# Third-level products in five more places, and the mixed kernels' operations handed out by a table

## The chip, the cores and the metric

The kernel runs on one core of one Trainium2 chip. The metric is the device time of one launch in microseconds (us); a core's engines are TensorE (PE for its matmuls, PEld for its weight loads), VectorE (DVE), ScalarE (ACT), GpSimd (POOL) and SyncE (SP, which here only issues transfers).

## The reference

Two layers work on `x` (32 samples, 128 channels, length 2048), all in float32:

```python
x = x + L0_ffn(L0_cond(x, cond))       # mixes channels per sample, then a 2048 x 2048 linear map along the length
x = x + L1_ffn(L1_cond(x, cond))       # grouped convolution of 9 taps, then 16 heads of up, gelu, down on permuted positions

# L0_cond:  att = softmax(mlp(cond));  out_b = (sum_k att[b,k] * weight[k]) @ x_b + att @ bias_k
# L0_ffn:   out = x @ W.T + bias + sum_e coeffs[e]*scales[e] * (x @ A[e].T) @ Bf[e].T
# L1_cond:  conv1d(x, weight, groups=4, padding=4) + cond @ c_weight.T + bias
# L1_ffn:   t = x[:, perm] as 16 heads of 128;  t = gelu(t @ up) @ down;  inverse permutation
```

The part that matters here is the linear map: 4096 rows (sample and channel) by 2048 by 2048, with the low-rank update folded into the weights first. Mixing the channels and the map along the length act on different axes, so the kernel does the map first and mixes its result. The mixing matrix of a sample (128 x 128, a sum of 8 given ones weighted by `att`) is its *mixed kernel*.

## The kernel before, in words

**Two levels of products, and a third in places.** The large product is done with the seven-product scheme (four sums of each operand, seven products P1 to P7, in place of eight). On the outside the 4096 rows are 8 groups `g` of 512, and each group's rows, the 2048 inputs and the 2048 outputs are halved. `ROUNDS` gives the order of the seven outer products: P1, P2, P6, P7, P5, P3, P4. A round keeps one set of weights (`rhs`) and goes through the eight groups; a step is one (round, group), and there are 56. In a step the same scheme is used again: 256 rows by 1024 by 1024 in seven products, each of 128 rows, 512 inputs and 512 outputs: four matmuls of 128 x 512, accumulated in a bank of PSUM. `multiply` (L341) does this. After each inner product DVE adds the bank to one or two places of the step's sum, `accs`, which is loaded from and stored to DRAM (`part_load`, `part_store`; `ADDED` says which sums a round adds to: two in P5, one in the others). Because a product accumulates onto a bank that held an earlier one (P6 and P7 on P1's, P3 on P5's), PE can start it only when DVE has read the bank.

**Third level.** For a pair of steps (g even, then g odd) listed in `PAIRS`, the inner products P2 and P4 of both steps are taken together: 256 rows by 512 by 512, done by seven *quarters*, each for P2 and P4 at once: four matmuls of 128 x 256 into the two halves of a bank (28 half-wide matmuls where 16 wide ones were). `multiply_third` (L575) does such a step; the even step leaves P2 and P4 out, the odd one has all the quarters. In the rounds of `ENDS` (P1 and P4) the quarters come behind the step's own products, otherwise among them. `MORE` lists pairs that do the same with the inner P3 and P7 (a second *family* of quarters): `multiply_more` (L482). There the even step already does P1 and P2 of both families, and the odd step the other ten quarters, the last ones in the order P7 of the second family, P4 of the first, P3 and P4 of the second. A quarter of the first family costs DVE one add of two halves (128 x 2 x 256) for each sum, one of the second also one of 128 x 256 (L527, L532).

**Inputs of the quarters.** `third_weights` (L388) makes eight sums of the weights on POOL and four on DVE (`quarter_ops`, done at points of the next steps); `more_weights` (L444) eight on POOL and eight on DVE (`more_ops`). `third_inputs` (L422) makes four sums of the two steps' x (two at once, two left in `rest` for later, if it runs on DVE); `more_inputs` (L463) four on POOL.

**Order of work.** The engines' queues are written by hand (`manual_schedule`), in the loop over `steps` (L1222). Before a step's matmuls come its loads, POOL's sums for the next step (`x_combine`), the loads of the next sums, and the weights of the next round (`outer_weights`, `inner_weights`). Inside a step six *points*, `between(0)` to `between(5)` (L1287), hang other work between the products; in the even step of a second-family pair, point 2 is behind P6 and points 3 to 5 among the quarters, in the odd step likewise. What hangs there: at points 0 to 3 of a step two of a mixed kernel's eight operations (`mixed_kernel`, L712 and L714, on DVE: 128 x 128, result = given matrix x att + result), one sample per step, in steps 6 and 7 of the first round and 1 to 6 of the later ones; at points 0 to 3 the waiting `quarter_ops` and `more_ops`; in the first round the row sums of the weights (`row_sums`, and for the first four weight tiles two adds at point 5 of each step). In the first round the other weights are also made, two tiles ahead of a step (`w_make_two`, L218).

**Buffers.** All large tiles share one pool of 26 slots of 1 MB (`SLOTS`); a load waits until its slot is free, and loads stand in one queue on SP. PSUM has 8 banks, taken and given back in turn.

In the last round (P4) the second layer begins between the products; after it PE runs the heads (L986, L997) to the end.

Of the kernel before, what the change touches and what calls it, by code (L numbers as in the profile page):

```python
# [48 lines left out]


PAIRS = {
    "P1": (1, 2, 3), "P2": (0, 1, 2, 3), "P6": (0, 1, 2, 3), "P7": (0, 1, 2, 3),
    "P5": (0, 1, 2, 3), "P3": (0, 1, 2, 3), "P4": (0,),
}
MORE = {"P7": (1, 2), "P3": (1, 2)}
ENDS = ("P1", "P4")
EARLY = 2

# [2 lines left out]
def adaln_ffn_kernel(  # L61
# [357 lines left out]

    rest = []  # L420

    def third_inputs(i, eng):  # L422

        (x11, x12), (x21, x22) = (
            [xa[n][:, 1, :, h * NQ : (h + 1) * NQ] for h in range(2)] for n in (i, i + 1)
        )
        tt = eng.tensor_tensor
        t = slot(f"sq_{i}", (P, 4, 2, NQ))
        tt(t[:, 0], x21, x22, ALU.add)
        tt(t[:, 1], t[:, 0], x11, ALU.subtract)  # L430
        rest.append((t[:, 2], x11, x21))
        rest.append((t[:, 3], x12, t[:, 1]))
        if eng is nc.gpsimd:
            sums_rest(eng)
        return {
            "P1": x11, "P2": x12, "P3": t[:, 3], "P4": x22,
            "P5": t[:, 0], "P6": t[:, 1], "P7": t[:, 2],
        }

    def sums_rest(eng):  # L440
        while rest:
            eng.tensor_tensor(*rest.pop(0), ALU.subtract)

    def more_weights(name, rhs):  # L444

# [36 lines left out]
    def multiply_more(r, g, lhs, rhs, accs, between, families):  # L482

        px, py = bank(), bank()
        if g % 2 == 0:
            both = [accs]
            held.extend((both, {}, {}))
        both, *sums = held
        if g % 2:
            both.append(accs)  # L490

        def add(ps, *to):
            for si, oi in to:
                for acc in accs:
                    nc.vector.tensor_tensor(acc[:, si, oi], ps, acc[:, si, oi], ALU.add)  # L495

        def product(k, ps, first, last):
            for kc in range(4):
                nc.tensor.matmul(  # L499
                    ps, lhsT=lhs[k][:, bass.ts(kc, P)], rhs=rhs[k][kc],  # L500
                    start=first and kc == 0, stop=last and kc == 3, skip_group_check=True,
                )

        def quarter(n, k):

            quarters, x = families[n]
            qs = sums[n]
            if k in ("P1", "P5", "P2"):
                qs[k] = bank()
            ps = qs[{"P6": "P1", "P7": "P1", "P4": "P1", "P3": "P5"}.get(k, k)]  # L510
            first, last = k in ("P1", "P2", "P5"), k in ("P2", "P3", "P4")
            for i, out in enumerate(halves(ps)):
                for kc in range(2):
                    nc.tensor.matmul(  # L514
                        out, lhsT=x[k][:, 1 - i if n else i, bass.ts(kc, P)],
                        rhs=quarters[i][k][kc],
                        start=first and i == 0 and kc == 0, stop=last and i == 1 and kc == 1,
                        skip_group_check=True,
                    )
            b, h = {  # L520
                "P1": (0, 0), "P2": (0, 0), "P6": (0, 1), "P5": (1, 1), "P7": (1, 1),
                "P3": (0, 1), "P4": (1, 0),
            }[k]
            cols = slice(h * NQ, (h + 1) * NQ)
            for acc in both[b]:
                part = acc[:, :, n, cols]
                nc.vector.tensor_tensor(  # L527
                    part, ps.rearrange("p (s n) -> p s n", s=2), part, ALU.add
                )
                if n:  # L530
                    part = acc[:, 1, 0, cols]
                    nc.vector.tensor_tensor(part, ps[:, NQ : 2 * NQ], part, ALU.add)  # L532
            if last:
                done(ps)

        def quarters_of(*nks):
            if g % 2:
                for n, k in nks:
                    quarter(n, k)

        product("P1", px, True, False)
        add(px, (0, 0))
        between(0)
        quarters_of((0, "P6"), (0, "P5"))
        product("P5", py, True, True)
        add(py, (1, 1), (0, 1))
        done(py)
        between(1)
        quarters_of((1, "P6"), (0, "P7"))
        product("P6", px, False, True)  # L550
        add(px, (0, 1), (1, 1), (1, 0))
        done(px)
        between(2)
        if g % 2 == 0:
            quarter(0, "P1")
            quarter(0, "P2")
            between(3)
            quarter(1, "P1")
            between(4)
            quarter(1, "P2")  # L560
            between(5)
            return
        quarters_of((1, "P5"), (0, "P3"))
        between(3)
        quarters_of((1, "P7"), (0, "P4"))
        between(4)
        quarters_of((1, "P3"))
        between(5)
        quarters_of((1, "P4"))
        held.clear()  # L570
        for b, accs in enumerate(both):
            for (_, new), acc in zip(ADDED[r], accs):
                part_store(new, g - 1 + b, acc, nc.sync)
# [639 lines left out]
    olds = {}  # L1213
    chain = small()
    nxt, waiting, ts, quarter_ops, more_ops = {}, {}, {}, [], []
    heads = [(g, h) for g in range(NG) for h in range(NH)]

    def olds_load(i):
# [3 lines left out]
    for i, (r, g) in enumerate(steps):  # L1222
        ri = i // NG
        last_round = ri + 1 == len(ROUNDS)
        if i + 1 < len(steps):
            if i + 1 not in xs:
                xs[i + 1] = x_loads(*steps[i + 1])
            if not last_round:
                lhs[i + 1] = x_combine(*steps[i + 1], xs.pop(i + 1))
                if g == 2 * PAIRS[r][0]:  # L1230
                    quarters, quarter_ops = third_weights(r, rhs)
                if in_pair(r, g) and g % 2 == 0 and g > 0 and r != "P6":
                    sq = third_inputs(i, nc.gpsimd)
                    if in_more(r, g):
                        sv = more_inputs(i)
                if r in MORE and g == 2 * MORE[r][0] - 1:
                    more, more_ops = more_weights(r, rhs)
        if i == 0:
# [48 lines left out]
        def between(j):  # L1287

            if j == 3 and 0 <= k_early < EARLY:
                outer_sums(k_early, early_x)  # L1290

            b = (ri - 1) * (NG - 2) + g + 1 if ri > 0 else g - (NG - 2)
            if (g in range(1, NG - 1) if ri > 0 else g >= NG - 2) and b < B:
                k = j - 2 if r == "P5" and g == 1 else j
                if 0 <= k < KEXP // 2:
                    mixed_kernel(b, (2 * k, 2 * k + 1))
            if ri == 0 and j == 2:
                for k in blocks[6 + 2 * g : 8 + 2 * g]:
                    wt[k] = w_load(*k)
            if j < 4 and quarter_ops:  # L1300
                nc.vector.tensor_tensor(*quarter_ops.pop(0), ALU.subtract)
            if j < 4 and more_ops:
                nc.vector.tensor_tensor(*more_ops.pop(0), ALU.subtract)
            if i == NG - 1 and j == 3:
                olds_load(i + 1)
            if j == 3 and ahead and steps[i + 2][0] == "P6":
                xs[i + 2] = x_loads(*steps[i + 2])
            if ri == 0 and j in (1, 3) and unsummed:
                row_sums(*unsummed.pop())
            if ri == 0 and j == 5 and unsummed_first:  # L1310
                t = unsummed_first.pop(0)
                tt = nc.vector.tensor_tensor
                tt(wsum[:, 0, 0], wsum[:, 0, 0], t[:, 0, 0], ALU.add)
                tt(wsum[:, 0], wsum[:, 0], t[:, 1], ALU.add)
            if last_round:
                if j == 1 and i + 1 < len(steps):
                    lhs[i + 1] = x_combine(*steps[i + 1], xs.pop(i + 1))
                    olds_load(i + 1)
                if j == 4 and i + 2 < len(steps):
                    xs[i + 2] = x_loads(*steps[i + 2])  # L1320
                if j in (2, 4):
                    stage(k0 + j // 2, stage_first)
                if j % 2:
                    stage_third(k0 + j // 2)
                else:
                    stage(k0 + j // 2, stage_second)
# [10 lines left out]
            multiply(r, g, lhs.pop(i), rhs, olds.pop(i), between)  # L1337
        xa.pop(i - 1, None)
        ss.pop(i - 1, None)
        if in_pair(r, g) and g % 2 == 0 and (g == 0 or r == "P6" or last_round):  # L1340
            sq = third_inputs(i, nc.gpsimd if r in ENDS else nc.vector)
        next(chain, None)
        if i > 4:
# [6 lines left out]
        if g == NG - 1 and ri + 1 < len(ROUNDS):  # L1350
            rhs = nxt
            nxt = {}

    before = None
    for k, (g, h) in enumerate(heads):
# [83 lines left out]
```

## Time and profile before

| | us |
|---|---|
| three runs | 2575.98, 2577.21, 2579.15 (median 2577.21) |
| the profiled execution | 2577.27 |
| its span, first to last instruction | 2575.5 |
| PE busy | 2564.0 |
| DVE busy | 1579.5 |
| POOL busy | 1394.2 |
| ACT busy | 532.3 |

The profile's lines name an engine, a line of the kernel, the tiles as output<-input, and counts. A group's line ends with its busy time, the mean of one instruction in ns and the idle time before it. In the timeline the first number is the start from the span's beginning, the second the time to the end of the last of the merged instructions, and what stands in brackets at the end is the idle time before and who ended it. Each matmul of float32 leaves two records there (7142 for 3571 instructions). The granted TensorE clock was 0.999 of full over the execution.

The rounds stand in the trace at these times: P1 from 45.9 us, P2 from 296.4, P6 from 482.8, P7 from 669.4, P5 from 853.1, P3 from 1038.8, P4 from 1222.5. An even step of a pair takes 17.2 us, an odd one 29.3 (27.6 to 28.9 with a second family).

### The profile page before, as it was taken

The numbers are of one execution on the slowest core, as the hardware profiler recorded it, in microseconds if no ns is written. First come the engines' busy times: TensorE is split into PE (matmuls) and PEld (weight loads), VectorE is DVE, ScalarE is ACT, GpSimd is POOL, SyncE is SP. The second block draws the span as 40 slices with busy tenths as digits, with TensorE's granted clock in tenths as the row PEclk, the third lists the DMA queues.
The fourth block names the chain that finished last, engine by engine and source line by source line (L and its number), as shares of the span: only waits on it lengthen the run. The fifth ranks groups of instructions, "written<-read, shape, count | busy, mean of one in ns | idle before, by whom it ended". The sixth has DMA issues, their size and how long they took to land.

```text
span 2575.5 us, 22121 instructions
## 1 busy us (share of the span) xinstructions
PE 2564.0 (100%) x7142; PEld 1355.4 (53%) x7142; DVE 1579.5 (61%) x2450; ACT 532.3 (21%) x1099; POOL 1394.2 (54%) x1158
## 2 busy tenths in 40 slices
PE   9999999999999999999999999999999999999999
PEld 4455555555566555566554554455555554455543
DVE  5665576666585576675476666666666666667611
ACT  0000000000000000000011244444444444444432
POOL 7431788878997736989432134444344434434222
PEclk9999999999999999999999999999999999999999
DMA  7452588579366486574866887787777877777432
GB/s 322 182 211 113 198 338 344 212 285 370 151 249 263 196 337 273 221 287 168 281 230 210 279 290 266 224 259 230 226 223 234 252 246 223 222 251 237 164 123 90
DMA packets 186867, 610.42 MB, mean 237 GB/s; under 512 B 17664, under 2 KB 91904, under 8 KB 142336
## 3 DMA queue, kind: packets, MB, share of 16 engines
q1 hardware_dynamic: 147936, 473.48, 51.2%
q0 software_dynamic: 32992, 132.14, 15.2%
q10 hardware_dynamic: 5824, 3.40, 0.5%
q8 instruction: 57, 0.93, 0.1%
q14 instruction: 58, 0.48, 0.1%
HBM read 372.45 MB, written 202.94 MB: 223 GB/s over the span
## 4 chain that ended last, share of the span: by engine, by line
PE 95%; DVE 3%; DMA 2%; issue 0%; SPq 0%; POOLq 0%; ACT 0%; ACTq 0%; DVEq 0%
PE bank L594 26%; PE bank L986 17%; PE bank L997 17%; PE bank L607 9%; PE bank L357 7%; PE bank L842 6%; PE bank L750 4%; PE bank L499 3%; PE bank L223 3%; PE bank L514 2%; DMA w<-in_WT 1%; DVE ags L714 1%; DMA xt<-in_xT 0%; DVE u L527 0%; DVE u L495 0%
## 5 line engine op out<-in xcount | busy, mean ns | idle before, releaser
L986 PE MATMUL bank<-t,ws 128*128 128x512 f32 x1024 | 460.3, 592 | 0.0
L997 PE MATMUL bank<-gl,ws 128*128 128x512 f32 x1024 | 460.1, 592 | 0.0
L1004 POOL DMA_INDIRECT out<-t,orow x128 | 152.3, 1189 | 535.8 <-DVE t L1002 452.5
L989 ACT ACTIVATE gl<-bank 128x512 f32<-128x512 f32 x512 | 306.1, 598 | 433.3 <-PE bank L986 414.1
L997 PEld LDWEIGHTS bank<-gl,ws 128*128 128x128 f32 x1024 | 194.6, 190 | 232.9 <-issue 231.5
L986 PEld LDWEIGHTS bank<-t,ws 128*128 128x128 f32 x1024 | 194.6, 190 | 226.6 <-issue 222.2
L594 PE MATMUL bank<-P_t,s_P 128*128 128x512 f32 x640 | 284.3, 592 | 0.4 <-ACT m_P L589 0.4
L1002 DVE TENSOR_TENSOR t<-bank,t 128x512 f32<-128x512 f32 x128 | 88.4, 690 | 320.2 <-PE bank L997 309.4
L735 POOL TENSOR_TENSOR x<-x,fb 128x512 f32<-128x512 f32 x128 | 174.5, 1392 | 198.9 <-DMA x<-in_x 136.4
L741 ACT ACTIVATE bank<-w,aggb 128x512 f32<-128x512 f32 x128 | 80.8, 684 | 880.3 <-DMA w<-w_d 867.8
L283 POOL TENSOR_TENSOR xt<-xt,xt 128x512 f32<-128x512 f32 x120 | 159.0, 1358 | 104.6 <-DMA xt<-in_xT 88.4
L714 DVE SCALAR_TENSOR_TENSOR ags<-mix,att_bc,ags 128x128 f32<-128x128 f32 x224 | 195.5, 873 | 4.7
L594 PEld LDWEIGHTS bank<-P_t,s_P 128*128 128x128 f32 x640 | 121.4, 190 | 140.4 <-issue 136.6
L587 DVE TENSOR_TENSOR u<-bank,u 128x512 f32<-128x512 f32 x156 | 101.6, 686 | 147.4 <-PE bank L594 135.1
L594 PE MATMUL bank<-wo_P,s_P 128*128 128x512 f32 x416 | 184.7, 592 | 0.0
L319 POOL TENSOR_TENSOR s_P<-xt 128x512 f32<-128x512 f32 x52 | 68.8, 1323 | 204.0 <-DMA xt<-in_xT 164.2
L970 POOL DMA_INDIRECT t<-hx_d,row x128 | 131.1, 1025 | 56.6 <-issue 25.6
L587 DVE TENSOR_TENSOR p<-bank,p 128x512 f32<-128x512 f32 x96 | 64.6, 687 | 117.8 <-PE bank L594 117.1
L594 PEld LDWEIGHTS bank<-wo_P,s_P 128*128 128x128 f32 x416 | 79.0, 190 | 89.2 <-issue 87.3
L842 PE MATMUL bank<-va,tw_l 128*128 128x256 f32 x512 | 121.5, 380 | 0.7 <-DVE va L826 0.7
L853 ACT ACTIVATE cv<-bank,ctxb 128x128 f32<-128x128 f32 x256 | 73.0, 368 | 234.6 <-PE bank L842 234.6
L753 DVE TENSOR_TENSOR x<-bank,x 128x512 f32<-128x512 f32 x128 | 88.1, 690 | 50.8 <-POOL x L735 21.9
(242 smaller groups left out, 3869.0 us busy)
## 6 DMA issues: line engine op xcount, KB each, us to landing
xt<-in_xT SPq DMA_DIRECT2D x84, 1024.0 KB
u<-u_d SPq DMA_DIRECT2D x40, 1024.0 KB
wo_P<-wb_d SPq DMA_DIRECT2D x36, 1024.0 KB
u<-c_d SPq DMA_DIRECT2D x64, 512.0 KB
x<-in_x SPq DMA_DIRECT2D x32, 1024.0 KB
xg<-x SPq DMA_DIRECT2D x256, 128.0 KB
hx_d<-x1t SPq DMA_DIRECT2D x32, 1024.0 KB
hx_d<-ht SPq DMA_DIRECT2D x32, 1024.0 KB
```

The source lines that it names most:

```text
L283: nc.gpsimd.tensor_tensor(out[:, i, j], a[:, i, j], b[:, i, j], op)
L357: nc.tensor.matmul(ps, lhsT=lhs[k][:, bass.ts(kc, P)], rhs=rhs[k][kc], start=first and kc == 0, stop=last and kc == 3, skip_group_check=True,)
L587: nc.vector.tensor_tensor(to, ps, to, ALU.add)
L594: nc.tensor.matmul(ps, lhsT=lhs[k][:, bass.ts(kc, P)], rhs=rhs[k][kc], start=first and kc == 0, stop=last and kc == 3, skip_group_check=True,)
L607: nc.tensor.matmul(out, lhsT=sq[k][:, i, bass.ts(kc, P)], rhs=quarters[i][k][kc], start=first and i == 0 and kc == 0, stop=last and i == 1 ...
L714: nc.vector.scalar_tensor_tensor(ag, mix[:, k], att, ag, ALU.mult, ALU.add)
L735: nc.gpsimd.tensor_tensor(xt[:, f], xt[:, f], late["fb"][:, f], ALU.add)
L842: nc.tensor.matmul(out, lhsT=w[:, 2 * i + r], rhs=rhs, start=first and r == 0, stop=last and r == 1, skip_group_check=True,)
L986: nc.tensor.matmul(pu, lhsT=w[:, m * P : (m + 1) * P], rhs=t[:, 0], start=True, stop=True)
L989: nc.scalar.activation(gl[m], pu, AF.Gelu)
L997: nc.tensor.matmul(pd, lhsT=w[:, (MC + m) * P : (MC + m + 1) * P], rhs=gl[m], start=(m == 0), stop=(m == MC - 1),)
L1004: nc.gpsimd.indirect_dma_start(out=out, out_offset=bass.IndirectOffsetOnAxis(ap=orow[:, g, h : h + 1], axis=0), in_=t[:, 1], in_offset=None,)
```

## The change

- `PAIRS`: P1's first pair (groups 0 and 1) now has the third level too, so all pairs of that round have it.
- `MORE`: a second family in one pair of P6 and of P5 (groups 2 and 3), and in the last pairs of P7 and P3 (groups 6 and 7), beside the two pairs each that P7 and P3 had.
- `MIXES`: the mixed kernels' operations are handed out by a table. For each round it has eight counts (operations per point in each of the eight groups) and eight first points; four points in a row get the count. The operations go in order through a list, `mixes`. The second-family pairs' even steps get 1 per point in place of 2 (none in P5's), the odd step of P5's pair 1 per point from point 2 on, and steps 7 of P2, P6, P7 and P5, which had none, 2 per point.
- `third_inputs`: all four sums go through `rest`; for P6's new pair none is made at once: two are made behind the even step, and two inside the odd step (`sums_rest`). Its input sums stay on DVE; `more_inputs` runs for the new pairs on POOL as for the old.
- In the first round, the row sums and the adds for the first four weight tiles stand at other points; the first pair's weight differences are made at step 0.

In the program that is 2306 matmuls of 128 x 512 in place of 2386, and 1318 of 128 x 256 in place of 1178; DVE has 42 more adds of 128 x 2 x 256, 51 more operations of 128 x 256 and two fewer of 128 x 512; POOL 20 more of 128 x 512 and 16 more of 128 x 256; SP's 742 transfers and the number of mixed-kernel operations stay.

```diff
 PAIRS = {
-    "P1": (1, 2, 3), "P2": (0, 1, 2, 3), "P6": (0, 1, 2, 3), "P7": (0, 1, 2, 3),
+    "P1": (0, 1, 2, 3), "P2": (0, 1, 2, 3), "P6": (0, 1, 2, 3), "P7": (0, 1, 2, 3),
     "P5": (0, 1, 2, 3), "P3": (0, 1, 2, 3), "P4": (0,),
 }
-MORE = {"P7": (1, 2), "P3": (1, 2)}
+MORE = {"P6": (1,), "P7": (1, 2, 3), "P3": (1, 2, 3), "P5": (1,)}
+MIXES = {
+    "P1": ((0,) * 8, (0,) * 8), "P2": ((0, 2, 2, 2, 2, 2, 2, 2), (0,) * 8),
+    "P6": ((0, 2, 1, 2, 2, 2, 2, 2), (0,) * 8), "P7": ((0, 2, 1, 2, 1, 2, 2, 2), (0,) * 8),
+    "P5": ((0, 2, 0, 1, 2, 2, 2, 2), (0, 2, 0, 2, 0, 0, 0, 0)),
+    "P3": ((0, 2, 1, 2, 1, 2, 2, 2), (0,) * 8), "P4": ((0,) * 8, (0,) * 8),
+}
...
-    def third_inputs(i, eng):
+    def third_inputs(i, eng, later=False):
...
-        tt(t[:, 0], x21, x22, ALU.add)
-        tt(t[:, 1], t[:, 0], x11, ALU.subtract)
-        rest.append((t[:, 2], x11, x21))
-        rest.append((t[:, 3], x12, t[:, 1]))
+        rest.append((t[:, 0], x21, x22, ALU.add))
+        rest.append((t[:, 1], t[:, 0], x11, ALU.subtract))
+        if not later:
+            sums_rest(eng, 2)
+        rest.append((t[:, 2], x11, x21, ALU.subtract))
+        rest.append((t[:, 3], x12, t[:, 1], ALU.subtract))
         if eng is nc.gpsimd:
             sums_rest(eng)
...
-    def sums_rest(eng):
-        while rest:
-            eng.tensor_tensor(*rest.pop(0), ALU.subtract)
+    def sums_rest(eng, n=4):
+        for _ in range(min(n, len(rest))):
+            eng.tensor_tensor(*rest.pop(0))
...
         quarters_of((0, "P6"), (0, "P5"))
+        if g % 2:
+            sums_rest(nc.vector)
         product("P5", py, True, True)
...
+    mixes = [(b, k) for b in range(2, B) for k in range(KEXP)]
...
-                if in_pair(r, g) and g % 2 == 0 and g > 0 and r != "P6":
-                    sq = third_inputs(i, nc.gpsimd)
-                    if in_more(r, g):
-                        sv = more_inputs(i)
+                if in_pair(r, g) and g % 2 == 0 and g > 0:
+                    if r != "P6":
+                        sq = third_inputs(i, nc.gpsimd)
+                    elif in_more(r, g):
+                        sq = third_inputs(i, nc.vector, True)
+                if in_more(r, g) and g % 2 == 0:
+                    sv = more_inputs(i)
...
-            if (g in range(1, NG - 1) if ri > 0 else g >= NG - 2) and b < B:
-                k = j - 2 if r == "P5" and g == 1 else j
-                if 0 <= k < KEXP // 2:
-                    mixed_kernel(b, (2 * k, 2 * k + 1))
+            if ri == 0 and g >= NG - 2 and j < KEXP // 2:
+                mixed_kernel(b, (2 * j, 2 * j + 1))
+            if 0 <= j - MIXES[r][1][g] < 4:
+                for _ in range(MIXES[r][0][g]):
+                    if mixes:
+                        b, k = mixes.pop(0)
+                        mixed_kernel(b, (k,))
...
-            if j < 4 and quarter_ops:
+            if i and j < 4 and quarter_ops:
...
-            if ri == 0 and j in (1, 3) and unsummed:
+            if ri == 0 and unsummed and (j in (1, 3) and (i, j) != (1, 3) or (i, j) == (3, 2)):
                 row_sums(*unsummed.pop())
-            if ri == 0 and j == 5 and unsummed_first:
+            if (i, j) in ((2, 5), (3, 0), (3, 4), (4, 0)) and unsummed_first:
...
-        if in_pair(r, g) and g % 2 == 0 and (g == 0 or r == "P6" or last_round):
+        if in_more(r, g) and r == "P6":
+            sums_rest(nc.vector, 2)
+        elif in_pair(r, g) and g % 2 == 0 and (g == 0 or r == "P6" or last_round):
             sq = third_inputs(i, nc.gpsimd if r in ENDS else nc.vector)
```

More of the change, by code (lines that the diff above doesn't have):

```diff
@@ L1352, in adaln_ffn_kernel @@
             nxt = {}
+    assert not mixes
     before = None
```

## The prediction

> **What bounds the kernel now.** First the page: its span, its busy line, and the chain that ended last.
>
> ```profile
> span 2575.5 us, 22121 instructions
> PE 2564.0 (100%) x7142; PEld 1355.4 (53%) x7142; DVE 1579.5 (61%) x2450; ACT 532.3 (21%) x1099; POOL 1394.2 (54%) x1158
> PE 95%; DVE 3%; DMA 2%; issue 0%; SPq 0%; POOLq 0%; ACT 0%; ACTq 0%; DVEq 0%
> ```
>
> TensorE is never out of work, so next what one matmul costs: the timeline of PE in a step of a pair with both families of quarters.
>
> ```profile
> 1102.43 3.60 PE L499 MATMUL bank<-wo_P,xt 128*128 128x512 f32 x8
> 1105.87 3.62 PE L514 MATMUL bank<-P_q,sq 128*128 128x256 f32 x16
> 1109.32 1.02 PE L499 MATMUL bank<-P_t,s_P 128*128 128x512 f32 x2
> ```
>
> A matmul leaves two records. From start to start eight wide records take 3.44 us and sixteen half-wide ones 3.45, so 0.859 us for a wide matmul and 0.431 for a half-wide one. The program's 2386 wide and 1178 half-wide matmuls make 2050 + 508 = 2558 us: only about 18 us of the span are anything else. Which waits these are, the PE's list of waits says:
>
> ```profile
> PE bank L514 <- DVE u L532: 1.1, 2, 0.8
> PE bank L514 <- DVE u L527: 0.5, 1, 0.5
> ```
>
> Both stand in pairs of this kind (starts late at 745.67, 760.10, 1128.50 and 1174.30; with the pipe's refill 0.75, 0.63, 0.33 and 1.02 us, 2.73 in sum). The last one, on DVE and then PE:
>
> ```profile
> 1164.95 1.88 DVE L495 TENSOR_TENSOR u<-bank,u 128x512 f32<-128x512 f32 x3 [1.53 <-PE bank L499]
> 1166.75 2.60 DVE L714 SCALAR_TENSOR_TENSOR ags<-mix,att_bc,ags 128x128 f32<-128x128 f32 x2
> 1169.27 0.68 DVE L527 TENSOR_TENSOR u<-bank,u 128x512 f32<-128x512 f32 x1
> 1169.87 0.41 DVE L532 TENSOR_TENSOR u<-bank,u 128x256 f32<-128x256 f32 x1
> 1170.20 0.68 DVE L527 TENSOR_TENSOR u<-bank,u 128x512 f32<-128x512 f32 x1
> 1170.80 2.51 DVE L714 SCALAR_TENSOR_TENSOR ags<-mix,att_bc,ags 128x128 f32<-128x128 f32 x2
> 1173.23 0.68 DVE L527 TENSOR_TENSOR u<-bank,u 128x512 f32<-128x512 f32 x1
> 1173.84 0.41 DVE L532 TENSOR_TENSOR u<-bank,u 128x256 f32<-128x256 f32 x1
> 1174.30 1.99 PE L514 MATMUL bank<-P_v,s_P 128*128 128x256 f32 x8 [0.76 <-DVE u L532]
> ```
>
> I call this the tail of an odd step. From P6's end PE has five quarters (8.6 us) until P4 of the second family needs its bank read; DVE has the adds of P6 and of three quarters (4.34 us by these cadences: 0.60, 0.60 and 0.33) and in between the mixed-kernel operations of two points, four of them here. These depend on POOL:
>
> ```profile
> 907.82 0.73 DVE L714 SCALAR_TENSOR_TENSOR ags<-mix,att_bc,ags 128x128 f32<-128x128 f32 x2
> 549.20 11.31 POOL L283 TENSOR_TENSOR xt<-xt,xt 128x512 f32<-128x512 f32 x8 [18.34 <-DMA xt<-in_xT]
> 920.05 4.99 POOL L283 TENSOR_TENSOR xt<-xt,xt 128x512 f32<-128x512 f32 x4 [23.40 <-DMA xt<-in_xT]
> ```
>
> At 907.8 POOL is idle and one costs 0.37 us; in the tail POOL runs one sum behind the other and one costs 1.24.
>
> **The change, part by part.** The profiled execution took 2577.27 us (its span and 1.77 around it), 0.06 over the median of the three runs, 2577.21; I sum against it.
>
> *Matmuls.* Five more uses of the third level: P1's first pair, and a second family in a pair of P6, P7, P5 and P3. Each drops 16 wide matmuls for 28 half-wide ones: 80 x 0.859 = 68.7 us against 140 x 0.4315 = 60.4. PE has **8.3 us** less.
>
> *DVE, P7 and P3.* The even steps of their old second-family pairs get 4 mixed-kernel operations in place of 8. In P7's step 3 DVE starts 5.4 us behind PE (P1's add begins at 741.85, its product ended at 736.4), the 0.75 us at 745.67. Four operations at 1.25 fewer take 5 us of that lag: **-0.75**. The odd steps keep eight, two per point, so the tails stay: 0.63, 0 (P7's step 5, where POOL paused and four cost 2.9), 0.33 and 1.02, a mean of 0.5. Such odd steps are now six (P6's 3, P7's 3, 5 and 7, P3's 3 and 5; P3's 7 has no mixed-kernel work): 6 x 0.5 = 3.0 in place of 1.98, **+1.0**. Ends: 0, if POOL pauses in each, and 1.1 each, if all four cost 1.27.
>
> *P5's pair.* Each add goes to two sums, so the tail's DVE work doubles: 6 x 0.60 + 1.87 + 1.2 + 1.87 + 0.1 = 8.6 us, which alone is over the 8.4 that PE leaves, plus two mixed-kernel operations (now one per point, from point 2). Stall 0.3 + 2m: 1.0 at m = 0.37, 2.8 at 1.27. In P5's step 3 the trace has POOL working through this stretch and eight of them took 8.8 us, so m = 1.1 and **+2.5**. Nearly all that this pair saves (1.66) is lost here. A rule of the Trainium skill (SBUF — State Buffer, Who interferes with whom: a VectorE instruction with two SBUF inputs and a GpSimd instruction that reads SBUF exclude each other, the second blocking until the first has finished) would make m a whole POOL sum, 1.27, and this +2.8; the trace's eight stay below it on the mean. Behind the pair DVE is some 4 us late in step 4, whose P6 waits only for P1's add, 6.9 us in: no cost.
>
> *P6's pair.* Its first two input sums are now queued on DVE behind the even step's last adds and needed 3.4 us into the odd step. Counting DVE's queue with four mixed-kernel operations and four weight differences (L1303: 1.48 beside POOL, 0.41 without), the adds end 0.9 us into the odd step and the sums (0.68 to 1.6 each) at 2.3 to 4.1: 0 to 0.7, taken 0, since POOL is idle there (18.34 us before 549.20).
>
> *P1.* Row sums leave point 5 of step 3, where they and the small chain delay the first adds of the weights (0.54 us at 181.42). One of two such waits goes (the other, 0.28 at 139.22, stays, as step 2 keeps its point 5): **-0.5**. Bounds: -0.8, and +1 for sums put in other places.
>
> *POOL* gets per new family 8 weight differences x 0.76 (P6 and P5 alone) and 4 input sums x 1.30: 11.2 us ahead of P7 and as much ahead of P3. It has the 18.3 and 23.4 us of waiting for loads shown above: nothing. *Queues*: the same 742 transfers leave SP; two more buffers in use in P6 and P5, and the quarters' in P1, make some loads start later. The tightest is a weight of P1 (w_111): its buffer now comes free with PE's step 1, about 15 us before its first add, where it was 35; a load into an idle queue (400's x: issued 139.9, first summed 145.3) took 5.4. The removed zero-mix steps (P2's, P6's, P7's, P5's step 7) have DVE at 9 to 18 of 29 us: 8 operations x 1.1 fit.
>
> Sum: -8.3 - 0.75 + 1.0 + 2.5 - 0.5 = -6.05: **2571.2 us**.
>
> **Rivals.**
>
> *All of it arrives.* POOL pauses in the tails and P5's two mixed-kernel operations cost 0.37: 1.0 + 6 x 0.33 in stalls, 3.0 against 2.73: -8.3 + 0.3 - 0.5 = -8.5, 2568.8. For it: P7's step 5. Against: three tails of four.
>
> *DVE's mixed-kernel work eats it.* Every one of these operations waits out a POOL sum, 1.27: six tails x 1.1 + 2.8 = 9.4 against 2.73, so -8.3 + 6.7 - 0.5 = -2.1, 2575.2. For it: the tail shown above; against: the other three (1.07, 1.06 and 0.73 each). It is what the Trainium skill's rule on the shared port (the page and section above) tends to where POOL's work has no gap; one tail of four agrees with it in full.
>
> *Slower: a half-wide matmul comes dearer than half.* Each needs its own weight load (190 ns against 216 ns of matmul). The place is the 140 new matmuls; it decides from 0.491 us on (68.7 / 140), and at three quarters of a wide one (0.64) they cost 90 us: +21 + 2.3, some 2600. Against it: the fence above, 0.431, with loads hidden. The Trainium skill (TensorE: Matmul & The Clock Gate, Back-to-back issue gap) states that in a stream of weight load and matmul the spacing falls from 131 ns at 512 columns only to 81 at 128, which would be such a price; this trace contradicts it, with 430 and 216 ns.
>
> *Slower: POOL's waits don't absorb its new work.* Then the 11.2 us come off POOL's lead on PE, which is 8.0 us at P7's step 1 and 6.2 at P3's (end of the weight difference to PE's first read): 3.2 + 5.0 lost, 2579.4, and over 2582 if POOL's sums run at 1.41 (the 11.31 us line) and not 1.27.
>
> **How the numbers follow.** The sum 0.50 (own range 2569.5 to 2573.5), all arrives 0.23, mixed-kernel work 0.18, dearer half-wide matmuls 0.02, POOL 0.07. A difference under 0.2%, 5.2 us, can't be told from none. Faster by more: 0.38 of the first and all of the second, 0.61; within: the rest of the first, the third, and 0.02 of POOL's, 0.32; slower 0.07. The range leaves out the two slower rivals and the ends of the others: 2567.5 to 2576.5.
>
> **What would show it.** PE's records: 2306 and 1318 matmuls, 0.859 and 0.431 us. No late start in P7's step 3 at the first family's P7; one of 1 to 3 us at the last quarter of P5's step 3; six tails of 0 to 1.1. POOL's gaps before P6's fourth and P5's third inputs shrunk by some 5 to 11 us. Wrong if PE waits for POOL or a load anywhere in P6 to P3, or if a tail costs over 3 us.

## The result, and the profile after

The changed kernel's median is 2573.2 us (22 runs, 2570.6 to 2575.0), that of the kernel before, beside it on the same chip, 2577.7 us: a ratio of 0.9982, 95% interval 0.9976 to 0.9988. It is faster, by 4.5 us: the interval leaves out 1, but the gain is a little less than the 0.2% (5.2 us) that the prediction set as its bound, so that its "faster by more", at 0.61, did not come, and its "within", at 0.32, did. Predicted were 2571.2 us and a range of 2567.5 to 2576.5, in which the time lies. The profiled execution took 2574.09 us against 2577.27, 3.2 less.

First the page: its span, its busy line and the chain that ended last.

```profile
span 2572.3 us, 22495 instructions
PE 2556.4 (99%) x7262; PEld 1377.8 (54%) x7262; DVE 1642.9 (64%) x2541; ACT 532.4 (21%) x1099; POOL 1435.0 (56%) x1194
PE 95%; DVE 4%; DMA 0%; issue 0%; POOLq 0%; ACTq 0%; ACT 0%; DVEq 0%
```

PE is still what fills the span; DVE has one per cent more of the chain than before. What a matmul costs has not moved, as PE's timeline in P3's step 3 shows (start, duration, line, matmul records):

```profile
1100.13 3.60 PE L507 MATMUL bank<-wo_P,xt 128*128 128x512 f32 x8
1103.57 3.62 PE L522 MATMUL bank<-P_q,sq 128*128 128x256 f32 x16
1107.02 3.60 PE L507 MATMUL bank<-P_t,s_P 128*128 128x512 f32 x8
```

Eight wide records again take 3.44 us from start to start and sixteen half-wide ones 3.45. The program has 2306 wide and 1318 half-wide matmuls. What changed is PE's list of waits; these four of its lines bear on the change (line, releaser: us in total, times, longest):

```profile
PE bank L522 <- DVE u L540: 2.1, 3, 1.0
PE bank L229 <- DVE w L232: 2.0, 1, 2.0
PE bank L507 <- DVE u L503: 1.5, 1, 1.5
PE bank L522 <- DVE p L540: 0.2, 1, 0.2
```

The first and last lines are the tails that the prediction spoke of. The second and third are new, one wait each, at places where it had costed nothing: in P1 at 140.39 us and between P5's steps 1 and 2 at 904.42.

A second reading gives each late start with the pipe's refill, as in the prediction: the gap from one PE record's start to the next, less 0.429 us for a wide record and 0.216 for a half-wide one (a record that runs slower counts in it, too). Summed by stretch, and beside it the matmul time at these steps:

| kernel | median us | matmuls | to 60 us | 60 to 290 (P1) | 290 to 1225 (P2 to P3) | behind |
|---|---|---|---|---|---|---|
| before | 2577.7 | 2557.7 | 2.8 | 2.3 | 3.5 | 0.9 |
| changed | 2573.2 | 2549.5 | 2.8 | 3.8 | 6.2 | 1.8 |

Matmuls give 8.24 us, and late starts take 5.05 back, 4.2 of them in P1 to P3. The first and the last stretch are not touched by the change; over all eleven profiles of this study they lie between 2.5 and 4.9 and (leaving out the one kernel that adds work there) between -0.2 and 3.2. Two profiles can differ by over 3 us from these alone, and so the places are read below from the middle columns.

**P1's new wait.** DVE's timeline of the changed kernel at that place, and SP's issues of the two weights' loads, before and then changed (start, time from the first issue to the end of the last, line):

```profile
139.65 3.68 DVE L232 TENSOR_TENSOR w<-bank,w 128x512 f32<-128x512 f32 x6 [2.58 <-DMA w<-in_WT]
```
```profile
107.69 4.34 SPq L164 DMA_DIRECT2D w<-in_WT  x2
```
```profile
110.95 23.91 SPq L170 DMA_DIRECT2D w<-in_WT  x2
```

DVE waits for a load of a weight. Before, both loads had left SP by 112 us; now the second, of the weight w_113, leaves at 134.9. What SP waited for in 104 to 143 us (total, times, longest), and POOL's issues of the stores to DRAM of the two weights made just before:

```profile
SPq L170 <- DMA wb_d<-w: 40.6, 2, 23.1
```
```profile
125.89 1.10 POOL L174 DMA_DIRECT2D wb_d<-w  x2
```

For 23.1 us the load waits for a store. In the program as built it goes into the buffer of w_111, and that is free only when w_111 has been stored; POOL issues this store behind its input sums. Before, the load went into a buffer of `m_P`, which was free by 112. The cause is the row sums of one other weight, w_012: the change moves them from step 1's point 3 to step 3, so that in step 2 its buffer is still taken, and each tile from there on gets another buffer than it would have had.

**P5's new wait.** DVE and, below it, POOL at the end of P5's step 1 in the changed kernel:

```profile
898.89 0.29 DVE L722 TENSOR_SCALAR ags<-mix,att_bc 128x128 f32<-128x128 f32 x1
899.21 3.86 DVE L724 SCALAR_TENSOR_TENSOR ags<-mix,att_bc,ags 128x128 f32<-128x128 f32 x3
903.00 1.27 DVE L503 TENSOR_TENSOR u<-bank,u 128x512 f32<-128x512 f32 x2
```
```profile
900.28 1.30 POOL L478 TENSOR_TENSOR sv<-s_P 128x512 f32<-128x512 f32 x1
901.67 1.26 POOL L479 TENSOR_TENSOR sv<-sv,s_P 128x512 f32<-128x512 f32 x1
902.89 1.31 POOL L480 TENSOR_TENSOR sv<-s_P,s_P 128x512 f32<-128x512 f32 x1
904.17 1.25 POOL L481 TENSOR_TENSOR sv<-s_P,sv 128x512 f32<-128x512 f32 x1
```

The last three of these mixed-kernel operations take 1.29 us each, and behind them stands the add of step 2's P1 (L503), for whose bank PE waits: 1.75 us late at 904.42. POOL's four sums are new, the input sums of P5's second family. Before, POOL was idle from 896.7 on.

### The profile page after: what moved, and what is told of

It is laid out like the page before. It is cut to its first block, busy times and chain, and to the rows that moved or that the text cites. A ratio compares the mean times of both kernels' runs of the same rounds, so it can differ in the third digit from the quotient of the medians.

```text
span 2572.3 us, 22495 instructions
## 1 busy us (share of the span) xinstructions
PE 2556.4 (99%) x7262; PEld 1377.8 (54%) x7262; DVE 1642.9 (64%) x2541; ACT 532.4 (21%) x1099; POOL 1435.0 (56%) x1194
## 4 chain that ended last, share of the span: by engine, by line
PE 95%; DVE 4%; DMA 0%; issue 0%; POOLq 0%; ACTq 0%; ACT 0%; DVEq 0%
PE bank L604 22%; PE bank L996 17%; PE bank L1007 17%; PE bank L617 8%; PE bank L852 6%; PE bank L522 6%; PE bank L507 6%; PE bank L363 5%; PE bank L760 4%; PE bank L229 3%; PE bank L186 1%; DVE ags L724 1%; DVE u L503 0%; DVE u L535 0%; DMA w<-in_WT 0%
## 5 line engine op out<-in xcount | busy, mean ns | idle before, releaser
L604 PE MATMUL bank<-P_t,s_P 128*128 128x512 f32 x544 | 241.4, 592 | 0.4 <-ACT m_P L599 0.4
L724 DVE SCALAR_TENSOR_TENSOR ags<-mix,att_bc,ags 128x128 f32<-128x128 f32 x224 | 206.7, 923 | 4.3
L604 PEld LDWEIGHTS bank<-P_t,s_P 128*128 128x128 f32 x544 | 103.3, 190 | 120.6 <-issue 116.9
L604 PE MATMUL bank<-wo_P,s_P 128*128 128x512 f32 x288 | 127.8, 592 | 0.0
L852 PEld LDWEIGHTS bank<-va,tw_l 128*128 128x128 f32 x512 | 97.0, 190 | 43.0 <-issue 32.1
L597 DVE TENSOR_TENSOR u<-bank,u 128x512 f32<-128x512 f32 x108 | 70.1, 686 | 77.9 <-PE bank L604 75.8
L597 DVE TENSOR_TENSOR p<-bank,p 128x512 f32<-128x512 f32 x84 | 56.6, 687 | 94.5 <-PE bank L604 93.2
```

What stands on the lines that cost most here:

```text
L604: nc.tensor.matmul(ps, lhsT=lhs[k][:, bass.ts(kc, P)], rhs=rhs[k][kc], start=first and kc == 0, stop=last and kc == 3, skip_group_check=True,)
L724: nc.vector.scalar_tensor_tensor(ag, mix[:, k], att, ag, ALU.mult, ALU.add)
L852: nc.tensor.matmul(out, lhsT=w[:, 2 * i + r], rhs=rhs, start=first and r == 0, stop=last and r == 1, skip_group_check=True,)
```

## The experiments

All are compared with the kernel before, run on the same chip beside them; the table of late starts goes on as above.

| kernel | median us | ratio to before, 95% interval | matmuls | to 60 us | 60 to 290 | 290 to 1225 | behind |
|---|---|---|---|---|---|---|---|
| row sums back | 2573.0 | 0.9981 (0.9972 to 0.9990) | 2549.5 | 3.4 | 2.3 | 7.7 | -0.2 |
| P5's step 1 empty | 2573.7 | 0.9983 (0.9974 to 0.9992) | 2549.5 | 2.7 | 3.4 | 6.2 | 1.7 |
| P5 with one family | 2573.5 | 0.9983 (0.9974 to 0.9992) | 2551.1 | 4.9 | 3.5 | 3.6 | 1.6 |
| old spread | 2582.5 | 1.0016 (1.0007 to 1.0025) | 2549.5 | 3.8 | 2.0 | 13.2 | 1.5 |
| new spread | 2568.2 | 0.9965 (0.9952 to 0.9979) | 2549.5 | 3.2 | 3.5 | 1.0 | 1.3 |
| P1 as before | 2574.7 | 0.9993 (0.9984 to 1.0002) | 2551.1 | 3.7 | 2.4 | 6.0 | 1.3 |
| changed spread alone | 2576.7 | 1.0002 (0.9993 to 1.0011) | 2557.7 | 2.5 | 2.4 | 2.2 | 0.2 |
| new spread, sums at point 5 | 2567.0 | 0.9955 (0.9942 to 0.9969) | 2549.5 | 3.1 | 1.6 | 1.1 | 3.2 |
| one more family in P6 | 2584.3 | 1.0023 (1.0014 to 1.0032) | 2547.8 | 3.1 | 1.6 | 15.7 | 6.0 |

**Row sums back at their points.**

```diff
-            if ri == 0 and unsummed and (j in (1, 3) and (i, j) != (1, 3) or (i, j) == (3, 2)):
+            if ri == 0 and unsummed and j in (1, 3):
```

> The row sums of P1's weights go back to points 1 and 3 of every step of the first round; all else is the changed kernel. Theory A (a buffer freed later): the second load of a weight left SP at about 134.5 us, right behind the row sums that freed its buffer, against 111.7 before. With the sums back at their point it leaves some 20 us earlier, the late start of 2.26 us at 140.4 goes, and up to 0.5 us comes back at another place of P1 (0.28 at 139.2 and 0.54 at 181.4 stood there before): 1.7 to 2.3 us shorter than the changed kernel, 2571 to 2572. Theory B (the transfer itself is slow, or its queue is taken by other loads): the late start stays within 0.5 us of 2.26, and so does the time.

The load leaves in time, once more into a buffer of `m_P`, and the late start at 140 is gone. SP, and DVE in step 1:

```profile
108.78 3.83 SPq L170 DMA_DIRECT2D w<-in_WT  x2
```
```profile
91.13 4.49 DVE L249 TENSOR_TENSOR wsum<-wsum,w 128x1024 f32<-128x1024 f32 x2
95.54 0.68 DVE L597 TENSOR_TENSOR m_P<-bank,m_P 128x512 f32<-128x512 f32 x1
```

But the sums now stand in the middle of the first pair's quarters: PE starts 0.71 us late at 96.96. P1 gains 1.55 us in sum, a little under the 1.7 to 2.3 expected. Theory A holds in that the place of the row sums decides; that they free the buffer, as it has it, does not: the load waits for the store. The median moved by only 0.2. In the profile, which is one run, P5's tail was 1 us dearer, in code that is the same; how that can be, the next experiment shows.

**P5's step 1 without mixed-kernel operations.**

```diff
-    "P5": ((0, 2, 0, 1, 2, 2, 2, 2), (0, 2, 0, 2, 0, 0, 0, 0)),
+    "P5": ((0, 0, 0, 1, 2, 2, 2, 2), (0, 0, 0, 2, 0, 0, 0, 0)),
```

> P5's step 1 gets no mixed-kernel operation; its eight move down the list, the last eight of the list to P3's step 7. Theory A (POOL's four new sums, 900.3 to 905.4 us, make the mixed-kernel operations on DVE dear just as DVE is to add P1): the late start of 1.75 us at 904.4 goes, P3's step 7 hides its eight operations at a cost of 0 to 0.7 us in its tail; 1.0 to 1.8 us shorter than the changed kernel. Theory B (the pair's own doubled adds and its eight weight differences hold DVE): at least 1.2 us of the 1.75 stay.

The 1.75 us at 904 went, as A had it, and P3's step 7 took the eight operations without a late start. The time did not follow: 2573.7. In the profile the tail of P5's step 3 rose from 1.26 to 2.33 us and that of P7's step 3 from 0.30 to 0.89. Both steps issue the same kinds of DVE and POOL instructions in the same order in both kernels. In P5's tail, changed kernel first and then this one, DVE's first operation of the two and the POOL sums around it:

```profile
935.84 0.35 DVE L724 SCALAR_TENSOR_TENSOR ags<-mix,att_bc,ags 128x128 f32<-128x128 f32 x1
939.15 0.77 DVE L724 SCALAR_TENSOR_TENSOR ags<-mix,att_bc,ags 128x128 f32<-128x128 f32 x1
```
```profile
934.61 1.28 POOL L325 TENSOR_TENSOR s_P<-xt 128x512 f32<-128x512 f32 x1
935.97 1.35 POOL L326 TENSOR_TENSOR s_P<-s_P,xt 128x512 f32<-128x512 f32 x1
```
```profile
934.30 1.33 DVE L724 SCALAR_TENSOR_TENSOR ags<-mix,att_bc,ags 128x128 f32<-128x128 f32 x1
938.61 0.84 DVE L724 SCALAR_TENSOR_TENSOR ags<-mix,att_bc,ags 128x128 f32<-128x128 f32 x1
```
```profile
934.22 1.27 POOL L325 TENSOR_TENSOR s_P<-xt 128x512 f32<-128x512 f32 x1
935.56 1.28 POOL L326 TENSOR_TENSOR s_P<-s_P,xt 128x512 f32<-128x512 f32 x1
```

In the changed kernel the operation starts just before the first sum ends (935.89), runs in 0.35 us, and the next sum is the one that takes longer (1.35). In this kernel it starts 0.08 us behind the sum's start and ends at 935.63, just behind the sum's end at 935.49: 1.33 us. A tenth of a microsecond in the phase of two engines decides over one microsecond of PE.

**P5's pair of steps 2 and 3 with one family.**

```diff
-MORE = {"P6": (1,), "P7": (1, 2, 3), "P3": (1, 2, 3), "P5": (1,)}
+MORE = {"P6": (1,), "P7": (1, 2, 3), "P3": (1, 2, 3)}
```

> P5's pair of steps 2 and 3 goes back to one family of quarters; the list of mixed-kernel operations stays. Theory A (this pair costs more than it saves): matmuls +1.66 us, the late starts of 1.75 us at 904.4 and 1.26 at 941.8 go: 1.35 us shorter than the changed kernel. Theory B (the pair pays; the waits belong to the mixed-kernel operations at these points and stay without it): 0.7 to 1.7 us longer.

Matmuls rose by 1.65 and both late starts (1.75 and 1.26) went. From P2 to P3 late starts fell by 2.6, so 0.95 net for theory A, less than its 1.35 as the tails of P7 came out 0.3 dearer; in the medians (+0.3) this is not to be seen, and the profile's first stretch alone was 2.2 us longer. The same mixed-kernel operations at the end of P5's step 1, now with POOL idle there:

```profile
900.69 0.28 DVE L722 TENSOR_SCALAR ags<-mix,att_bc 128x128 f32<-128x128 f32 x1
901.00 1.13 DVE L724 SCALAR_TENSOR_TENSOR ags<-mix,att_bc,ags 128x128 f32<-128x128 f32 x3
```

Three in 1.13 us, where the changed kernel had 3.86 beside POOL's sums. The 2.7 us between them is more than the late start of 1.75. With the run before this settles it: the operations alone hold PE up there, and they are dear because POOL's new sums run beside them.

**The old spread under the new pairs.**

```diff
-    "P6": ((0, 2, 1, 2, 2, 2, 2, 2), (0,) * 8), "P7": ((0, 2, 1, 2, 1, 2, 2, 2), (0,) * 8),
...
+MIXES = {r: ((0, 2, 2, 2, 2, 2, 2, 0), (0,) * 8) for r in ("P2", "P6", "P7", "P5", "P3")}
+MIXES |= {"P1": ((0,) * 8, (0,) * 8), "P4": ((0,) * 8, (0,) * 8)}
+MIXES["P5"] = (MIXES["P5"][0], (0, 2, 0, 0, 0, 0, 0, 0))
```

> All the pairs of the changed kernel with the mixed-kernel operations as they were spread before: two per point at points 0 to 3 of steps 1 to 6 of a round, in P5's step 1 from point 2 on. Theory A (each operation that DVE runs between the adds of a step of two families costs 0.4 to 1.2 us of its lag): the even steps 2 and 4 of P7 and P3, 2 of P6 and P5 and 4 of P7 again carry 8 in place of 4 or none; P7's step 3 has a late start of 0.75 us again at the first family's P7, P6's 0.5 to 1.5 more, and the tail of P5's step 3, with twice the operations, 1.26 + 2 x 0.56 = 2.4; against that P7's step 7 is freed and saves nothing: 2 to 4 us longer than the changed kernel. Theory B (DVE has slack enough, and the spread is worth nothing): within 0.7 us of the changed kernel.

2582.5 us: slower than before, and 9 us slower than the changed kernel, where I expected 2 to 4. In the profiles, which are 6.4 us apart, nearly all of it is one place: P5's step 3, whose late starts near 943 are 7.47 us in sum, where the changed kernel has 1.26. I had counted only the tail's two operations more. DVE's rows in P5's step 3:

```profile
930.23 1.98 DVE L721 SCALAR_TENSOR_TENSOR ags<-mix,att_bc,ags 128x128 f32<-128x128 f32 x2
938.77 2.36 DVE L721 SCALAR_TENSOR_TENSOR ags<-mix,att_bc,ags 128x128 f32<-128x128 f32 x2
944.12 1.21 DVE L721 SCALAR_TENSOR_TENSOR ags<-mix,att_bc,ags 128x128 f32<-128x128 f32 x2
```

None of DVE's rows between 917.6 and 945 names a wait: it comes out of step 2, which has eight operations here and none in the changed kernel, with a lag, has no pause to make it good, and every operation adds in full. In the changed kernel the same stretch has four waits of 0.20, 0.44, 2.15 and 1.35 us, 4.1 in sum, in which the lag of step 2 is lost. The 0.75 us of P7's step 3 did not come back; only its tail grew (1.15 against 0.30).

A part of the 7.47 us is not DVE's. PE behind its wait, and a stretch of 2 us there (busy time of each engine, and in the third place from the end the granted clock of PE):

```profile
943.14 3.75 PE L519 MATMUL bank<-wo_P,sv 128*128 128x256 f32 x8 [4.04 <-DVE u L537]
```
```profile
943.00:945.00 2.00, 1.86 (x5) 1.53 (x6) 1.97 (x4) 0.00 (x0) 1.79 (x2) 0.50 0.00 0
```

Eight half-wide records take 3.75 us here, where they take 1.89 elsewhere: after 4 us without work PE's granted clock was 0.50 for some 7 us. For the first of the two quarters this costs nothing, as PE waits for DVE again at 947.24; behind that it adds some 0.7 us. The wait of 2.0 us at 140.39 in the changed kernel left the clock at 1.00.

P1's column is 2.0 here though its code is that of the changed kernel: the load again waits for the store and leaves by 134.3, before the row sums at 132.25 to 134.7 are done, but PE runs 1.1 us later from the first stretch on, and only 0.4 us of the late start is left. So this late start, too, differs between two runs of one code.

**The changed spread alone, with the pairs of before.**

```diff
-    "P1": (0, 1, 2, 3), "P2": (0, 1, 2, 3), "P6": (0, 1, 2, 3), "P7": (0, 1, 2, 3),
+    "P1": (1, 2, 3), "P2": (0, 1, 2, 3), "P6": (0, 1, 2, 3), "P7": (0, 1, 2, 3),
...
-MORE = {"P6": (1,), "P7": (1, 2, 3), "P3": (1, 2, 3), "P5": (1,)}
+MORE = {"P7": (1, 2), "P3": (1, 2)}
```

(The row sums are as before, too.)

> The pairs of the kernel before with the changed spread of the mixed-kernel operations alone. Theory A (the spread only makes room for the new pairs): P7's late start of 0.75 us in step 3 goes, the tails stay; matmul time as before, 0.7 us shorter than before, 2576 to 2577.3. Theory B (the spread is worth something by itself, the new pairs little): 2573 to 2575.

2576.7 us, not to be told from before (interval 0.9993 to 1.0011), and the late starts of P2 to P3 fall from 3.5 to 2.2: theory A, the 0.75 us of P7 and half a microsecond in the tails. With the old spread under the new pairs this makes a square of four: the new pairs alone cost 5 us, the spread alone gives at most 1.4 (by the late starts; 0.4 by the medians, which is not to be told from nothing), and both together give 4.5. The gain of the pairs needs the spread.

**P1 as before.**

```diff
-    "P1": (0, 1, 2, 3), "P2": (0, 1, 2, 3), "P6": (0, 1, 2, 3), "P7": (0, 1, 2, 3),
+    "P1": (1, 2, 3), "P2": (0, 1, 2, 3), "P6": (0, 1, 2, 3), "P7": (0, 1, 2, 3),
...
+            if ri == 0 and unsummed and j in (1, 3):
+            if ri == 0 and j == 5 and unsummed_first:
```

> The changed kernel without P1's first pair, and with the sums of P1's weights where they were before: P1 as before, the rest as changed. Theory A (P1's part is worth nothing): matmuls +1.65 us, the late start of 2.26 at 140.4 goes, 0.28 at 139 and 0.54 at 181 come back: 0.2 us, between 0.8 shorter and 0.5 longer than the changed kernel. Theory B (P1's part pays as predicted): 2.1 us longer, because the late start at 140 belongs to the load and not to the sums' place, and stays.

Matmuls +1.65, late starts of P1 from 3.82 to 2.39: 0.2 us for the pair, as theory A has it. The medians (2574.7 and 2573.2) lie 1.5 apart and would also admit B, but the wait that B needs, 2 us at 140, is not there (0.41).

**A new spread.** If the late starts come from DVE's work between the adds of these steps, they must go where it goes.

```diff
-    "P6": ((0, 2, 1, 2, 2, 2, 2, 2), (0,) * 8), "P7": ((0, 2, 1, 2, 1, 2, 2, 2), (0,) * 8),
-    "P5": ((0, 2, 0, 1, 2, 2, 2, 2), (0, 2, 0, 2, 0, 0, 0, 0)),
-    "P3": ((0, 2, 1, 2, 1, 2, 2, 2), (0,) * 8), "P4": ((0,) * 8, (0,) * 8),
+    "P6": ((1, 2, 1, 1, 2, 2, 2, 2), (0,) * 8), "P7": ((0, 2, 1, 1, 1, 1, 2, 1), (0,) * 8),
+    "P5": ((0, 0, 0, 0, 2, 2, 2, 2), (0,) * 8),
+    "P3": ((1, 2, 1, 1, 1, 1, 2, 2), (0,) * 8), "P4": ((2, 2, 0, 0, 0, 0, 0, 0), (0,) * 8),
...
+            if ri == 0 and unsummed and ((i, j) == (1, 6) if i == 1 and j > 1 else j in (1, 3)):
```

(P2's step 0 gets one per point, too.)

> The pairs of the changed kernel, with the row sums of P1's step 1 at its point 6 and no longer in step 3, and the 240 mixed-kernel operations put elsewhere: none in P5's steps 1 and 3, one per point in place of two in the odd steps of the other second families (P6's 3, P7's 3, 5 and 7, P3's 3 and 5); the freed ones go to the steps 0 of P2, P6 and P3 and to P4's steps 0 and 1, where VectorE is busy 9 to 15 of 23 us. Theory A (the late starts come from VectorE's work at these places, and the places with slack take it for nothing): P1's 2.26 goes, P5's 1.75 goes and its tail falls from 1.26 to 2.3 to 0.3, the other tails (0.49, 0.30, 0.62, 0.26 and 0.97) to 0.2 or less each; 6.0 to 8.5 us shorter than the changed kernel, 2565 to 2568. Theory B (VectorE's lag only moves to the next place): late starts of 3 us or more at new places, 2569 to 2573.

2568.2 us, 9 us faster than before. Of the seven late starts from P6 to P3 one is left, P5's tail with 0.32 us at 937.94: the 0.3 that the prediction's formula leaves at no mixed-kernel operation at all. In P7's step 3, first the changed kernel and then this one:

```profile
750.64 1.86 DVE L724 SCALAR_TENSOR_TENSOR ags<-mix,att_bc,ags 128x128 f32<-128x128 f32 x2
753.95 2.52 DVE L724 SCALAR_TENSOR_TENSOR ags<-mix,att_bc,ags 128x128 f32<-128x128 f32 x2
756.40 0.68 DVE L535 TENSOR_TENSOR u<-bank,u 128x512 f32<-128x512 f32 x1
```
```profile
750.36 0.72 DVE L724 SCALAR_TENSOR_TENSOR ags<-mix,att_bc,ags 128x128 f32<-128x128 f32 x1
752.61 0.98 DVE L724 SCALAR_TENSOR_TENSOR ags<-mix,att_bc,ags 128x128 f32<-128x128 f32 x1
755.46 0.69 DVE L535 TENSOR_TENSOR u<-bank,u 128x512 f32<-128x512 f32 x1 [0.70 <-PE bank L522]
```

With two operations in place of four DVE gets to the quarters ahead of PE and waits for it. The late start of P1 stayed (1.93): a pair's step has only points 0 to 5, so that point 6 is never reached, and w_012 kept its buffer still.

**The same, with those sums at point 5.**

```diff
+            if ri == 0 and unsummed and ((i, j) == (1, 5) if i == 1 and j > 1 else j in (1, 3)):
```

> The last spread (no mixed-kernel operation in P5's steps 1 and 3, one per point in the odd steps), with the row sums of P1's step 1 at its point 5, the last that a pair's step reaches (a pair's step has points 0 to 5, so point 6 was never reached there, and the sums stayed one weight behind). Theory A (a buffer freed later makes the load at 140 late): the load leaves SP some 20 us earlier, the late start falls from 1.93 to the 0.4 that stands where the sums are made at point 3, and the sums, 2.5 to 4.5 us on VectorE with only the last quarter and the next weights behind them, cost 0 to 0.7: 0.8 to 1.5 us shorter than the last spread. Theory B (the sums are as dear here as at point 3): a new late start of 0.7 us or more between 100 and 115 us, and the time within 0.8 us of the last spread.

2567.0 us, ratio 0.9955: the best of the study, 11 us faster than before and some 6 faster than the changed kernel. DVE, and SP:

```profile
103.77 2.47 DVE L249 TENSOR_TENSOR wsum<-wsum,w 128x1024 f32<-128x1024 f32 x2
106.16 0.68 DVE L625 TENSOR_TENSOR m_P<-bank,m_P 128x512 f32<-128x512 f32 x1
```
```profile
107.81 4.29 SPq L170 DMA_DIRECT2D w<-in_WT  x2
```

The sums of w_012 are done at 106.2, so that its buffer can be given to others in step 2, and the load, again into a buffer of `m_P`, leaves by 112. No late start over 0.15 us is left in P1 before the small chain of 176, neither at 140 nor at 97. P1's late starts fall by 1.9 against the spread before it, more than the 0.8 to 1.5 expected. The medians of the two lie 1.2 apart.

**One more second family, in P6's steps 4 and 5.**

```diff
-MORE = {"P6": (1,), "P7": (1, 2, 3), "P3": (1, 2, 3), "P5": (1,)}
+MORE = {"P6": (1, 2), "P7": (1, 2, 3), "P3": (1, 2, 3), "P5": (1,)}
...
+    "P6": ((1, 2, 1, 1, 1, 1, 2, 2), (0,) * 8), "P7": ((0, 2, 1, 1, 1, 1, 2, 1), (0,) * 8),
+    "P3": ((1, 2, 1, 1, 1, 1, 2, 2), (0,) * 8), "P4": ((3, 3, 0, 0, 0, 0, 0, 0), (0,) * 8),
```

> The same, and a second family in P6's pair of steps 4 and 5 as well, with one mixed-kernel operation per point in both; the eight freed go to P4's steps 0 and 1 (three per point). Theory A (a family is worth its matmuls, 16 x 0.859 - 28 x 0.4315 = 1.66 us, where VectorE has room): 1.3 to 1.66 us shorter than the kernel without it. Theory B (VectorE or POOL has no room for one more): late starts of 1.5 us or more in P6's steps 4 and 5 or in P4's steps 0 and 1, and nothing gained.

2584.3 us, 17 more than without it: on B's side, and far beyond it. One wait of PE makes most of it, for P6's input sums on DVE, which wait for POOL:

```profile
PE bank L522 <- DVE sq L450: 11.4, 1, 11.4
```
```profile
601.47 1.73 DVE L450 TENSOR_TENSOR sq<-xt 128x512 f32<-128x512 f32 x1 [10.31 <-POOL wo_P L289]
```
```profile
595.29 1.26 POOL L481 TENSOR_TENSOR sv<-s_P,sv 128x512 f32<-128x512 f32 x1
596.51 4.92 POOL L289 TENSOR_TENSOR wo_P<-wo_P,wo_P 128x512 f32<-128x512 f32 x4
```

DVE's first sum is released when POOL has combined a weight of the next round, and POOL does that behind the four new input sums. The sums read nothing of that weight. In the program as built they take a buffer that this combining is the last to read. Behind the wait the granted clock of PE was 0.50 once more, until 609.3: the sixteen half-wide records from 604.92 on took 5.88 us in place of 3.62, 2.3 of the 17. With three operations per point in P4's steps 0 and 1 PE loses another 4 us there (late starts of 0.98, 2.62 and 0.38); with two there was no late start in these steps. Each family has its own buffers and queue places, and the price of one does not hold for the next.

## Why the prediction was right, and where it was not

The sum was -6.05 us; the profiles' own terms, in its order, are these.

- *Matmuls, -8.3:* 2557.69 to 2549.45 by the records, -8.24. Right. The rival of dearer half-wide matmuls is refuted: they stayed at 0.43 us. The spacings of the Trainium skill that stood beside it (TensorE: Matmul & The Clock Gate, Back-to-back issue gap) do not hold here: at a granted clock of 0.999 this trace has 0.429 us a record at 512 columns and 0.216 at 256, and not the page's 131 ns at 512.
- *P7's step 3, -0.75:* right; gone here and with the spread alone.
- *Six tails, +1.0:* 0.49, 0.30, 0.62, 0, 0.26 and 0.97 are 2.64 against 1.99 before, +0.65. Right in mechanism and about in size; with half the operations all six are gone.
- *P5's tail, +2.5:* 1.26 in this profile, and 2.29, 2.33 and 1.34 in the three others that have the step unchanged. 0.3 + 2m holds: 0.32 at no operation, and 0.35 + 0.77 and 1.33 + 0.84 us of operations give 1.42 and 2.47 by it. m is 0.56 to 1.09 and not fixed at 1.1: by which 0.1 us the first operation meets a sum. The Trainium skill's rule (SBUF — State Buffer, Who interferes with whom) agrees with the rows at 934 us, where the operation waits out the sum; its full price of 1.27 for each was not reached, as the second operation starts in the middle of a sum (0.75 to 0.84).
- *P6's input sums, 0:* right, no late start in P6's step 3 ahead of its tail.
- *P1, -0.5:* **the step that failed first.** 0.28 and 0.54 went (I had kept 0.28), but 2.26 came: +1.4. I had looked at the loads and called that of w_111 the tightest, its buffer freed by PE. The late one was that of w_113, into w_111's own buffer, which a store held until 134.5. I had costed the sums' move at their old and new place on DVE and not for the buffer that stays taken meanwhile, by which the loads behind come to other buffers. With the sums at point 5 the term would have been better than forecast (2.3 to 1.6, -0.7).
- *POOL's new work, nothing:* **the second that failed.** As stated it is true: POOL's waits took it (18.3 to 9.0 us, and 23.4 to 11.2 in the row below), its lead fell to no less than 4.5 us, PE waits for POOL nowhere, and the slower rival is refuted.

```profile
916.59 4.96 POOL L289 TENSOR_TENSOR xt<-xt,xt 128x512 f32<-128x512 f32 x4 [11.17 <-DMA xt<-in_xT]
```

But the pause that it filled was what kept DVE's operations of P5's step 1 cheap: 1.75 us late at 904. I had priced this collision in the tails alone, the rows of before showing it there, and not in the even steps, where only DVE's lag was counted.

- *P5's step 4 and the steps 7, nothing:* right; no late start in either.

These terms make -8.24 - 0.75 + 0.65 + 1.26 + 1.75 + 1.44 = -3.9; the profiles differ by 3.2, the rest being places that the change does not touch (among them +0.55 at the first matmul, -0.57 at 38 us, +0.90 at 2132). The medians give 4.5. So the forecast was 1.5 us (by the medians) to 2.9 (by the profiles) too fast, by two costs of 1.75 and 1.9 us that it had at nothing and by one, P5's tail, that came out up to 1.2 smaller. That the time still fell into the range is due to the range's width, and in part to luck: P5's tail, at its lowest in this profile, took back a third of what the two costs added. Of the rivals, mixed-kernel work did eat part of the gain, but mostly at another place and not by its price of 9.4 us in the tails; that everything arrives needed the new spread. (The rivals' 2568.8 and 2575.2 start from the profiled 2577.27, the sum from the median, 2577.21.)

## What to carry to other kernels

Work moved into another engine's pause is free for that engine and not for its neighbours: where two engines' operations exclude each other, price the pause at what it made cheap. When a step that reads a buffer last is moved, see which buffers the loads behind it now get, and what else holds these, whatever the step itself costs. And where a wait comes from small work standing between an engine's urgent steps, moving that work into a stage with slack can be worth as much (5 us here) as the change that had made it urgent (4.5).

## What was not expected of the hardware

An operation of 0.35 us on DVE takes 1.33 when it starts 0.08 us behind the start of a POOL sum, and 0.35 when it starts 0.05 us before a sum's end: identical code gave late starts of 1.26 to 2.33 us at the same place. PE waits of 4.0 and 11.4 us were followed by records at half pace, at a granted clock of 0.50, for some 4 to 6 us; the second of these waits cost 2.3 us more than itself.

The first stretch of the program, the same in all, varied from 2.5 to 4.9 us between the profiles, as much as half of what was to be measured; only reading by place made the terms comparable. Most of the surplus of the run with 4.9 (P5 with one family) is the same half pace:

```profile
6.63 5.56 PE L186 MATMUL bank<-bf_sb,a_sb 128*128 128x256 f32 x16 [0.53 <-DMA bf_sb<-in_BfT]
```

Sixteen half-wide records take 5.56 us here, and 3.62 later; in the changed kernel those from 6.30 us on were at full pace.
